# A four-layer graph network on one Trainium2 core: edge starts looked up in rows of 200 instead of 800, and a 6 MB store in seven pieces

## The chip, the core and the metric

The kernel runs on one core of one Trainium2 chip. That core has five engines that each work through their own instruction stream in order: TensorE (PE, matrix products), VectorE (DVE), ScalarE (ACT), GpSimd (POOL) and SyncE (SP, which here only issues transfers). Sixteen DMA engines move data between the chip's memory (HBM) and the core's on-chip memory. SP and ACT issue ordinary transfers; POOL issues the indirect ones, the gathers.

The metric is the time on the device in microseconds, from the start to the end of one execution. Before the change it was 6752.54 us, the median of three runs (6749.43 to 6761.02).

## The reference

There are 6250 nodes with 128 features and 100,000 edges (`src`, `dst`). The edges arrive **sorted by `dst`**. Four layers follow one another, each with a residual and a layer norm:

```python
edge_index = jnp.stack([src, dst])
x = _layernorm(x + _L0_gnn_ref(x, edge_index, ...))               # mean over incoming edges, two products, unit norm
x = _layernorm(x + _L1_gnn_ref(x, edge_weight1, ..., edge_type_8)) # one product per relation, weighted sum
x = _layernorm(x + _L2_gnn_ref(x, edge_index, ...))               # five gated steps (GRU), then an MLP
x = _layernorm(x + _L3_gnn_ref(x, edge_index, edge_attr_16, ...)) # edge MLP, sum by src, node MLP
```

The change touches the first layer only, and the preparation ahead of it:

```python
msg = x[src]
summed = jax.ops.segment_sum(msg, dst, num_segments=n)
cnt = jax.ops.segment_sum(jnp.ones((msg.shape[0],), x.dtype), dst, num_segments=n)
mean = summed / jnp.maximum(cnt, 1.0)[:, None]
out = mean @ W_l + b_l + x @ W_r
return out / jnp.maximum(norm, EPS)                               # norm: the length of each row of out
```

Because `dst` is sorted, the edges of a node are one stretch of the list. If the first edge of node n is first(n), its count is first(n+1) - first(n). So counts need no pass over the edges, only the first edge of each node: the number of `dst` entries below n.

## The kernel before

**Preparation** (`gnn_kernel`, lines 2089 to 2273). `dst` lies in on-chip memory as 125 rows of 800. The last entry of each row (`ends`) tells how many rows end below a given node; a product with a column of ones counts them (line 2133), and that is the row in which the node's first edge lies. Six gathers (line 2141) fetch that row for 6 x 128 nodes, an accumulating compare (`less`, line 2144) counts the entries below the node, and row x 800 + count is the first edge. These starts go to memory (`start_d`) and serve as addresses later. Beside it, x is cut into three bf16 parts in thirteen tiles (`xin`, lines 2254 to 2270), loaded through the SP queue.

**Layer 0** (`even`, lines 777 to 1156). Nodes are cut into steps of four and two tiles of 128. The eight steps of four tiles are *dense*: for each, a 6272 x 512 adjacency matrix of edge counts is built on chip (`stage`, two buffers), written to HBM for the five steps of layer 2 (`adj_d`), and multiplied with x. I call the work on one of them a *chunk*. The rest is *sparse*: its messages are gathered edge by edge (`m<-x_in`, 306 gathers).

The work of the four engines PE, DVE, ACT and POOL is in an order written out by hand: each piece is an event with a due time in units of one chunk, and `play` (line 720) emits the events sorted by it. SP is not among the four; its transfers are placed by the scheduler. A wait in one event holds up everything behind it on its engine. The events are:

- `subtile` (line 940): chunk d spends times d to d+1 on 43 subtiles of twelve nodes. `hot_keys` on DVE makes one-hot matrices `ohk` for one subtile ahead, PE multiplies them with `ohs` (`adj_p`, line 951), ACT copies the sums to `stage` (line 953).
- `block_load` and `block_keys` (lines 906 and 918): every eleven subtiles form a block. SP loads its edge records (`recs`, eleven small transfers), DVE makes `ohs` from them in one long instruction (line 928). The first two blocks are both loaded and keyed ahead of everything else.
- `stored` (line 957), at d+1: SP writes the whole `stage` to HBM in one transfer of 6272 KB.
- `dense0` (line 967), spread over d+1 to d+2: PE multiplies `stage` with x, whose parts `xs` come in groups of seven tiles through SP (`parts_load`, line 960, three buffers; the load of group g+3 is called when group g is used up). `post` then finishes the nodes of the chunk.
- `sparse0` (line 996): one product per gather; the gather is called eight products ahead (`fetch0`), with ten buffers.
- `counts` (line 840): for seven groups of 7 x 128 nodes, 0.37 apart and so within the first 2.7 chunks. `row` finds the row as above; `look` gathers it on POOL (128 rows of 3200 bytes, two buffers `grow`); `less` on DVE compares it, 0.095 of a chunk after its `look`; `first`, `following` and `inverse` make 1/count (`rc`), which `post` needs.

Of the kernel before, what the change touches and what calls it, by code (L numbers as in the profile page):

```python
# [8 lines left out]
F32 = mybir.dt.float32  # L9
BF16 = mybir.dt.bfloat16  # L10
# [5 lines left out]
P = 128  # L16
# [22 lines left out]
SLOTS = 18  # L39
NU = (N + U - 1) // U  # L40
QR = P - 1
NQ = 5 * QR
# [618 lines left out]
def even(ctx: ExitStack, tc: tile.TileContext, a, out, rec_d, start_d, list_d, x_in, ends):  # L661
# [115 lines left out]
    with tc.tile_pool(name="f0", bufs=1) as l0, \  # L777
# [39 lines left out]
        def list_locs(i):  # L817
# [10 lines left out]
        nc.gpsimd.iota(node7, pattern=[[1, CN * P]], base=0, channel_multiplier=0, allow_small_or_imprecise_dtypes=True)  # L828
        ends7 = l0.tile([EP, NT // CN], F32, name="ends7")
        nc.gpsimd.iota(ends7, pattern=[[-CN * P, NT // CN]], base=0, channel_multiplier=0,  # L830
                       allow_small_or_imprecise_dtypes=True)
        nc.vector.tensor_scalar(ends7, ends7, ends, None, op0=ALU.add)
        ones_c = l0.tile([P, 1], BF16, name="ones_c")
# [3 lines left out]
        nc.sync.dma_start(node_d[NPAD:].rearrange("(o p) -> o p", o=1), tail)  # L837
        dst_v = a["dst"].rearrange("(p c) -> p c", p=EP)

        def counts(b, at, to):  # L840
# [3 lines left out]
            def row():  # L844
                ended = l0.tile([EP, CN * P], BF16, tag="ended", name=f"ended{b}")
                nc.vector.tensor_scalar(ended, node7, ends7[:, b:b + 1], None, op0=ALU.is_gt)
                p = ps(f"row_p{b}")
                for j in range(CN):
                    nc.tensor.matmul(p[:, j:j + 1], ended[:, j * P:(j + 1) * P], ones_c[:EP, :], start=True, stop=True)
                v["row"] = row_f = l0.tile([P, CN], F32, tag="row_f", bufs=2, name=f"row_f{b}")  # L850
                nc.vector.tensor_scalar(row_f, p[:, :CN], float(EP - 1), None, op0=ALU.min)
                v["row_i"] = row_i = l0.tile([P, CN], I32, tag="row_i", bufs=2, name=f"row_i{b}")
                nc.vector.tensor_copy(row_i, row_f)
                v["in"] = l0.tile([P, CN], F32, tag="inrow", bufs=2, name=f"inrow{b}")

            def look(j):
                v[j] = g = l0.tile([P, EC], I32, tag="grow", bufs=2, name=f"grow{b}_{j}")
                gather(g, dst_v, v["row_i"][:, j:j + 1])
# [7 lines left out]
            def first():  # L866
                f = l0.tile([P, CN], F32, tag="first", name=f"first{b}")
                nc.vector.scalar_tensor_tensor(f, v["row"], float(EC), v["in"], op0=ALU.mult, op1=ALU.add)
                p = ps(f"first_p{b}")
                nc.tensor.transpose(p[:CN, :P], f, ident)  # L870
                v["T"] = fT = l0.tile([CN, P], F32, tag="firstT", bufs=3, name=f"firstT{b}")
                nc.vector.tensor_copy(fT, p[:CN, :P])
                nc.sync.dma_start(node_d[CN * P * b:CN * P * (b + 1)].rearrange("(t p) -> t p", p=P), fT)
# [16 lines left out]
            for j in range(CN):  # L890
                ev += [(at + 0.06 + 0.05 * j, lambda j=j: look(j)), (at + 0.155 + 0.05 * j, lambda j=j: less(j))]
            return ev + [(at + 0.50, first), (to + 0.12, following), (to + 0.24, inverse)]

# [62 lines left out]

        def stored(d):
            nc.sync.dma_start(adj_d[d].rearrange("p (t n) -> p t n", n=DW), stages[d][:, :NT, :])

# [141 lines left out]
        with tc.manual_schedule(engines=FOUR):  # L1101
            list_load(0)
            for i in range(2):
                block_load(i)
            list_load(1)
            load_weights()
            for i in range(2):
                block_keys(i)
            list_locs(0)
            for k in range(8):  # L1110
                fetch0(k)
# [7 lines left out]
            for d in range(len(dense)):  # L1119
                mine = [o for o in order if o[0] == d]  # L1120
                for k, (_, b, u) in enumerate(mine):
                    t = d + (k + 0.5) / len(mine)
                    g = order.index((d, b, u))
                    nxt = order[g + 1][1:] if g + 1 < len(order) else None
                    i = [x[1] for x in blocks].index(b)
                    if u == 0 and i:
                        events.append((t - 1e-6, lambda i=i: block_load(i + 1)))
                    if u == 7 and i:
                        events.append((t - 2e-6, lambda i=i: block_keys(i + 1)))
                    events.append((t, lambda d=d, b=b, u=u, nxt=nxt: subtile(d, b, u, nxt)))  # L1130
                events.append((d + 1, lambda d=d: stored(d)))
                for s in range(NT):
                    events.append((d + 1 + (s + 0.5) / NT, lambda d=d, s=s: dense0(d, s)))
                events += post(dense[d], d + 2.02, d + 2.95 if d < 7 else d + 2.5)
            for b in range(NT // CN):
                events += counts(b, 0.01 + 0.37 * b, 0.01 + 0.37 * min(b + 1, NT // CN - 1) + 0.50)
            for i in range(1, len(sparse)):
# [937 lines left out]
def gnn_kernel(ctx: ExitStack, tc: tile.TileContext, a, out):  # L2075
# [7 lines left out]
    x_in = dram.tile([NPAD, 3 * D], BF16, name="x_in")  # L2083
    ends = keep.tile([EP, 1], F32, name="ends")
    bad_i = keep.tile([1, 1], I32, name="bad_i")
# [3 lines left out]
    with tc.tile_pool(name="prep", bufs=1) as prep, \  # L2089
# [37 lines left out]
        nc.vector.tensor_copy(d_f, d_i)  # L2127
        nc.vector.tensor_copy(ends, d_f[:, EC - 1:EC])
        ended = prep.tile([EP, NR * P], BF16, name="ended")
        nc.vector.tensor_scalar(ended, node[:EP, :], ends, None, op0=ALU.is_gt)  # L2130
        p_r = psum.tile([P, 512], F32, name="p_r")
        for r in range(NR):
            nc.tensor.matmul(p_r[:, r:r + 1], ended[:, r * P:(r + 1) * P], ones_b[:EP, :], start=True, stop=True)
        row_f = prep.tile([P, NR], F32, name="row_f")
        nc.vector.tensor_scalar(row_f, p_r[:, :NR], float(EP - 1), None, op0=ALU.min)
        row_i = prep.tile([P, NR], I32, name="row_i")
        nc.vector.tensor_copy(row_i, row_f)
        inrow = prep.tile([P, NR], F32, name="inrow")
        for r in range(NR):
            g = prep.tile([P, EC], I32, tag="grow", bufs=NR, name=f"grow{r}")  # L2140
            nc.gpsimd.indirect_dma_start(out=g, out_offset=None, in_=dst_v,
                                         in_offset=bass.IndirectOffsetOnAxis(ap=row_i[:, r:r + 1], axis=0))
            less = prep.tile([P, EC], BF16, tag="less", bufs=2, name=f"less{r}")
            nc.vector.tensor_scalar(less, g, own[:, r:r + 1], 0.0, op0=ALU.is_lt, op1=ALU.add,
                                    accum_out=inrow[:, r:r + 1])
        first = prep.tile([P, NR], F32, name="first")
        nc.vector.scalar_tensor_tensor(first, row_f, float(EC), inrow, op0=ALU.mult, op1=ALU.add)
        p_t = psum.tile([P, 512], F32, name="p_t")
# [169 lines left out]
```

## Time and profile before

| what | value |
|---|---|
| median of three runs | 6752.54 us |
| the profiled execution: its time, and its span from first to last instruction | 6750.44 us, 6748.6 us |
| preparation, until the last write of `x_in` is issued | 0 to 72.6 us |
| first product of a subtile | 102.96 us |
| the eight stores of the adjacency are issued at | 174.1, 283.9, 391.8, 477.9, 559.9, 639.2, 722.2, 804.7 us |
| end of layer 0 (last product of `fhw_p`) | about 895 us |
| gathers `grow` in layer 0: count, first and last issue | 49, 103.8 and 352.9 us |

How to read it: the page names an instruction by line, engine, operation and the tiles it writes and reads ("out<-in"). Busy time is the time of the instructions themselves; idle time ahead of an instruction is put down to what released it ("<-"). The granted clock is the share of full speed that TensorE was allowed. Between two stores lies one chunk, so the table of stores is also a table of chunk lengths: 109.8 and 107.9 us for the second and third, 79.3 to 86.1 us for the later ones.

### The profile page before, as it was taken

Reading aid. Unit: us, or ns where it says so; the run is one execution under the profiler, and the core shown is the slowest. Engines: PE = TensorE matmul, PEld = TensorE weight load, DVE = VectorE, ACT = ScalarE, POOL = GpSimd, SP = SyncE. Lnnn points to the kernel's source line nnn. Section 1 sums busy time; section 2 is a strip of 40 time slices with the busy share of each in tenths; the row PEclk is TensorE's granted clock in tenths of the full one; section 3 lists DMA queues with packets and bytes.
Section 4 is the critical chain, followed back from the end, with each engine's and each line's share of the span. In section 5 each row is a group of like instructions: output and inputs, shape, how many; then the busy total and the mean of one; then the engine's idle time right before and its main releaser. Section 6 shows DMA issues by size and latency. Waiting matters only on the chain.

```text
span 6748.6 us, 83991 instructions
## 1 busy us (share of the span) xinstructions
PE 5859.5 (87%) x25874; PEld 4036.2 (60%) x25874; DVE 2935.8 (44%) x8837; ACT 2404.4 (36%) x3623; POOL 4285.6 (64%) x4463
## 2 busy tenths in 40 slices
PE   4689877789859889999999989999999987888888
PEld 2345445556546657666676667666676665566665
DVE  6676534466624422222222222222222235677776
ACT  2244411111126643333333333333333323444444
POOL 5555447777756656656666666666666622777775
PEclk7899976677769989999999999999999999999999
DMA  5788744444468888768777787778776743444443
GB/s 156 235 246 241 224 135 141 137 135 133 128 179 269 272 284 264 250 221 287 257 255 233 243 301 254 245 227 305 229 239 218 232 155 103 105 107 108 111 107 81
DMA packets 804341, 1358.23 MB, mean 201 GB/s; under 512 B 165559, under 2 KB 428845, under 8 KB 802860
## 3 DMA queue, kind: packets, MB, share of 16 engines
q1 hardware_dynamic: 548348, 693.60, 32.3%
q0 software_dynamic: 207952, 570.83, 28.5%
q10 hardware_dynamic: 47584, 88.33, 3.5%
q8 instruction: 212, 3.47, 0.2%
q14 instruction: 245, 2.01, 0.1%
HBM read 1048.97 MB, written 303.32 MB: 200 GB/s over the span
## 4 chain that ended last, share of the span: by engine, by line
PE 57%; DMA 22%; DVE 8%; issue 5%; POOL 4%; ACT 1%; SPq 1%; DVEq 0%; ACTq 0%; POOLq 0%; another core or an unknown queue 0%
PE ag_p L1445 17%; DMA m<-tab,src_l 7%; PE r L1529 5%; PE z L1529 5%; DMA f_m<-by_dst,f_ix 5%; PE sp_p L1477 4%; DMA fm<-f_hw,turned_hw 4%; PE sum L1366 4%; PE h L1529 3%; PE i L1529 3%; PE ag_p L972 3%; POOL f_m L752 2%; PE adj_p L951 2%; PE g_rank L2037 2%; DMA ab<-adj_d 1%
## 5 line engine op out<-in xcount | busy, mean ns | idle before, releaser
L1445 PE MATMUL ag_p<-af,hs 128*128 128x512 f32 x7056 | 2097.0, 421 | 85.5 <-DMA ab<-adj_d 36.1
L752 POOL DMA_INDIRECT m<-tab,src_l x1530 | 1476.6, 965 | 1055.4 <-PE ag_p L1445 507.5
L1445 PEld LDWEIGHTS ag_p<-af,hs 128*128 128x128 f32 x7056 | 1325.6, 193 | 493.5 <-issue 134.7
L1416 ACT CAST af<-ab 128x1024 fp32r<-128x1024 bf16 (+1 forms) x1000 | 1022.6, 1028 | 984.1 <-PE ag_p L1445 628.5
L752 POOL DMA_INDIRECT f_m<-by_dst,f_ix x819 | 792.2, 967 | 301.8 <-issue 168.2
L752 POOL DMA_INDIRECT fm<-f_hw,turned_hw x782 | 779.6, 997 | 249.1 <-issue 95.5
L1614 POOL DMA_INDIRECT rec_d<-f_rec,row x782 | 778.2, 995 | 237.9 <-issue 207.5
L1477 PE MATMUL sp_p<-m,s 128*128 128x512 f32 (+1 forms) x1530 | 682.3, 446 | 165.8 <-DMA m<-tab,src_l 160.0
L1467 DVE TENSOR_SCALAR s<-iota_h,loc_l 128x128 fp32r<-128x128 f16 x1530 | 421.7, 302 | 769.9 <-PE sp_p L1477 766.1
L1366 PE MATMUL sum<-fs,fm 128*128 128x128 f32 (+13 forms) x1924 | 461.4, 380 | 185.7 <-DMA fm<-f_hw,turned_hw 109.3
L1366 PEld LDWEIGHTS sum<-fs,fm 128*128 128x128 f32 x1924 | 377.1, 272 | 305.9 <-DVE fs L1357 128.1
L752 POOL DMA_INDIRECT m<-x_in,src_l x306 | 349.2, 1141 | 254.7 <-PE sp_p L1003 149.5
L1477 PEld LDWEIGHTS sp_p<-m,s 128*128 128x128 f32 x1530 | 294.5, 192 | 339.6 <-issue 192.7
L953 ACT CAST stage<-adj_p 128x600 bf16<-128x600 f32 (+1 forms) x344 | 224.5, 654 | 347.3 <-PE adj_p L951 313.7
L972 PE MATMUL ag_p<-stage,xs 128*128 128x512 bf16 x1176 | 330.2, 394 | 16.8 <-DMA xs<-x_in 13.4
L951 PE MATMUL adj_p<-ohk,ohs 128*128 128x300 bf16 x1376 | 251.5, 308 | 89.1 <-DVE ohk L936 88.1
L1543 DVE SCALAR_TENSOR_TENSOR r<-h,fc_b_hh,r 128x256 f32<-128x256 f32 (+2 forms) x170 | 101.7, 600 | 521.2 <-PE h L1529 456.4
L1860 ACT ACTIVATE f_hs<-dT,fc_eb 128x512 f32<-128x512 f32 (+1 forms) x208 | 148.8, 715 | 497.3 <-DVE dT L1858 497.3
L1551 ACT ACTIVATE z<-z,f_brz 128x256 f32<-128x256 f32 (+2 forms) x170 | 96.6, 568 | 592.0 <-PE z L1529 531.3
L1336 ACT COPY f_rec<-ap_p 128x512 f32<-128x512 f32 x196 | 105.1, 589 | 561.6 <-issue 335.6
L1357 DVE TENSOR_SCALAR fs<-f_iota_n,loc,turned_wgt 128x128 f32<-128x128 f32 x782 | 245.7, 360 | 92.0 <-PE sum L1366 91.1
L1560 DVE TENSOR_TENSOR r<-hold,ng 128x256 f32<-128x256 f32 (+2 forms) x153 | 84.4, 552 | 459.2 <-ACT ng L1553 459.2
(383 smaller groups left out, 9079.6 us busy)
## 6 DMA issues: line engine op xcount, KB each, us to landing
ab<-adj_d SPq DMA_DIRECT2D x960, 256.0 KB
f_rec<-edge_d SPq DMA_DIRECT2D x391, 130.0 KB
rg<-rec_d SPq DMA_DIRECT2D x195, 260.0 KB
edge_d<-f_rec SPq DMA_DIRECT2D x97, 520.0 KB
adj_d<-stage SPq DMA_DIRECT2D x8, 6272.0 KB
tab<-r ACTq DMA_DIRECT2D x196, 256.0 KB
hs<-tab SPq DMA_DIRECT2D x28, 1792.0 KB
xs<-x_in SPq DMA_DIRECT2D x56, 672.0 KB
```

The source lines that it names most:

```text
L752: nc.gpsimd.indirect_dma_start(out=dst, out_offset=None, in_=table, in_offset=bass.IndirectOffsetOnAxis(ap=idx, axis=0))
L951: nc.tensor.matmul(p[:, q * 512:q * 512 + KH * U], ohss[b][:, 2 * u + j, :], ohk[:, q * KH * U:(q + 1) * KH * U], start=(j == 0), stop=(j ...
L953: nc.scalar.copy(stages[d][:, :, c:c + w].rearrange("p (q b) d -> p q b d", q=2), p.rearrange("p (q n) -> p q n", q=2)[:, :, :KH * U] .rea ...
L972: nc.tensor.matmul(sums["d", d], parts[d, g][:, s % XG, q, :], stages[d][:, s, :], start=(s == 0 and q == 0), stop=(s == NT - 1 and q == 2))
L1357: nc.vector.tensor_scalar(s, iota_n, loc[:, k:k + 1], wgt[:, k:k + 1], op0=ALU.is_equal, op1=ALU.mult)
L1366: nc.tensor.matmul(sums[c][:, x0 - c0:x1 - c0], msg, s[:, x0 - w0:x1 - w0], start=False, stop=(k == last_k[c]))
L1416: nc.scalar.copy(af[:, :m, :], abs_.pop((layer, d, g))[:, :m, :])
L1445: nc.tensor.matmul(sums[layer, d, k], hs[:, s, q, k, :], afs[layer, d, g][:, s % SG, :], start=(s == 0 and q == 0), stop=(s == NT - 1 and ...
L1467: nc.vector.tensor_scalar(s, iota_h, loc_l[:, i, j:j + 1], None, op0=ALU.is_equal)
L1477: nc.tensor.matmul(p[:, :2 * w], hot.pop((layer, k)), msgs.pop((layer, k))[:, :2 * w], start=(j == 0), stop=(j == SLOTS - 1))
L1529: nc.tensor.matmul(p[:, :n], w[:, k, ms], src, start=(start and i == 0), stop=(stop and i == len(ks) - 1))
L1614: st = nc.gpsimd.indirect_dma_start(out=rec3_d, out_offset=bass.IndirectOffsetOnAxis(ap=row3[:, c:c + 1], axis=0), in_=recs[c // CB][:, c ...
```

## The change

Four edits in layer 0, and the first of them also in the preparation:

1. The rows of the look-up hold 200 entries instead of 800. There are now four times as many row ends, so `row` makes four compares instead of one (two buffers) and 28 products instead of seven, which add up in PSUM on top of a product with zeros. A gather brings 800 bytes per row instead of 3200, and `less` runs over 200 entries. In the preparation: four compares, 24 products, six gathers of 200.
2. `grow` has six buffers instead of two, and `less(j)` comes 0.28 of a chunk after `look(j)` instead of 0.095. `first` moves from 0.50 to 0.66, and `following` and `inverse` move with it.
3. `stored` writes seven groups of seven tiles (896 KB each), at d+1, d+1.13, ... d+1.78.
4. At the start only block 0 is keyed, after the first sparse list; the records of block 1 are loaded after the second list, and its keys are made at subtile 7 of block 0.

```diff
+RL = 200
+RQ = EC // RL
...
-        ends7 = l0.tile([EP, NT // CN], F32, name="ends7")
+        ends7 = l0.tile([EP, RQ, NT // CN], F32, name="ends7")
...
+        zero_c = l0.tile([P, CN], F32, name="zero_c")
+        nc.vector.memset(zero_c, 0.0)
...
-        dst_v = a["dst"].rearrange("(p c) -> p c", p=EP)
+        dst_v = a["dst"].rearrange("(r c) -> r c", c=RL)
...
             def row():
-                ended = l0.tile([EP, CN * P], BF16, tag="ended", name=f"ended{b}")
-                nc.vector.tensor_scalar(ended, node7, ends7[:, b:b + 1], None, op0=ALU.is_gt)
                 p = ps(f"row_p{b}")
-                for j in range(CN):
-                    nc.tensor.matmul(p[:, j:j + 1], ended[:, j * P:(j + 1) * P], ones_c[:EP, :], start=True, stop=True)
+                nc.tensor.matmul(p[:, :CN], ident, zero_c, start=True, stop=False)
+                for q in range(RQ):
+                    ended = l0.tile([EP, CN * P], BF16, tag="ended", bufs=2, name=f"ended{b}_{q}")
+                    nc.vector.tensor_scalar(ended, node7, ends7[:, q, b:b + 1], None, op0=ALU.is_gt)
+                    for j in range(CN):
+                        nc.tensor.matmul(p[:, j:j + 1], ended[:, j * P:(j + 1) * P], ones_c[:EP, :],
+                                         start=False, stop=(q == RQ - 1 and j == CN - 1))
...
             def look(j):
-                v[j] = g = l0.tile([P, EC], I32, tag="grow", bufs=2, name=f"grow{b}_{j}")
+                v[j] = g = l0.tile([P, RL], I32, tag="grow", bufs=6, name=f"grow{b}_{j}")
                 gather(g, dst_v, v["row_i"][:, j:j + 1])
...
             for j in range(CN):
-                ev += [(at + 0.06 + 0.05 * j, lambda j=j: look(j)), (at + 0.155 + 0.05 * j, lambda j=j: less(j))]
-            return ev + [(at + 0.50, first), (to + 0.12, following), (to + 0.24, inverse)]
+                ev += [(at + 0.06 + 0.05 * j, lambda j=j: look(j)), (at + 0.06 + 0.28 + 0.05 * j, lambda j=j: less(j))]
+            return ev + [(at + 0.66, first), (to + 0.12, following), (to + 0.24, inverse)]
...
-        def stored(d):
-            nc.sync.dma_start(adj_d[d].rearrange("p (t n) -> p t n", n=DW), stages[d][:, :NT, :])
+        def stored(d, g):
+            ts = slice(XG * g, XG * (g + 1))
+            nc.sync.dma_start(adj_d[d].rearrange("p (t n) -> p t n", n=DW)[:, ts, :], stages[d][:, ts, :])
...
             list_load(0)
-            for i in range(2):
-                block_load(i)
+            block_load(0)
             list_load(1)
+            block_load(1)
             load_weights()
-            for i in range(2):
-                block_keys(i)
             list_locs(0)
+            block_keys(0)
...
-                    if u == 7 and i:
+                    if u == 7:
                         events.append((t - 2e-6, lambda i=i: block_keys(i + 1)))
...
-                events.append((d + 1, lambda d=d: stored(d)))
+                for g in range(NT // XG):
+                    events.append((d + 1 + 0.13 * g, lambda d=d, g=g: stored(d, g)))
...
-                events += counts(b, 0.01 + 0.37 * b, 0.01 + 0.37 * min(b + 1, NT // CN - 1) + 0.50)
+                events += counts(b, 0.01 + 0.37 * b, 0.01 + 0.37 * min(b + 1, NT // CN - 1) + 0.66)
...
-        nc.vector.tensor_scalar(ended, node[:EP, :], ends, None, op0=ALU.is_gt)
+        for q in range(RQ):
+            ended = prep.tile([EP, NR * P], BF16, name=f"ended{q}")
+            nc.vector.tensor_scalar(ended, node[:EP, :], ends[:, q:q + 1], None, op0=ALU.is_gt)
+            eds.append(ended)
...
         for r in range(NR):
-            g = prep.tile([P, EC], I32, tag="grow", bufs=NR, name=f"grow{r}")
+            g = prep.tile([P, RL], I32, tag="grow", bufs=NR, name=f"grow{r}")
```

## The prediction

> **What bounds the kernel now.** The change ends with layer 0, so I read the first 900 us, and first by chunk: busy time of each engine from the first subtile to the first store, and between stores. Columns: length; busy us (instructions) of PE, weight loads, DVE, ACT, POOL; granted clock; DMA share; GB/s.
>
> ```profile
> 102.70:174.10 71.40, 43.07 (x223) 21.84 (x224) 59.28 (x164) 28.09 (x44) 47.49 (x42) 0.76 0.65 174
> 174.10:283.90 109.80, 77.55 (x405) 40.89 (x405) 76.77 (x219) 32.18 (x53) 62.89 (x59) 0.85 0.73 225
> 283.90:391.80 107.90, 82.32 (x430) 45.31 (x428) 77.03 (x229) 39.44 (x68) 58.65 (x53) 0.91 0.77 233
> 391.80:477.90 86.10, 79.78 (x433) 45.04 (x432) 57.81 (x180) 40.20 (x70) 45.17 (x39) 0.98 0.78 232
> 477.90:559.90 82.00, 75.85 (x414) 43.02 (x412) 55.92 (x175) 38.23 (x67) 44.58 (x37) 0.98 0.83 244
> ```
>
> From the fourth chunk on PE is busy 93% of the time and sets the pace. The first three hold the same kind of work, and in the second and third PE is idle for 26 to 32 us. They are the ones with the look-ups. The list of waits from 100 to 400 us (total, times, longest) says on what:
>
> ```profile
> PE adj_p L951 <- DVE ohk L936: 66.3, 28, 14.4
> DVE grow L863 <- DMA grow<-in_dst,row_i: 47.8, 11, 15.0
> POOL grow L752 <- DVE grow L863: 33.2, 10, 13.8
> ```
>
> PE waits for DVE's one-hots; DVE stands in `less` for a gather 47.8 us; POOL, with two buffers, stands for `less`, and its message gathers behind it. The two long waits follow a store directly. In the timeline (start, duration, idle before), with the store on SP's queue:
>
> ```profile
> 174.12 0.32 SPq L958 DMA_DIRECT2D adj_d<-stage  x1
> ...
> 175.01 0.94 POOL L752 DMA_INDIRECT grow<-in_dst,row_i  x1 [0.31 <-issue]
> ...
> 194.64 1.05 DVE L863 TENSOR_SCALAR_CACHE_REDUCE grow<-grow,own_n 128x800 int32<-128x800 int32 x1 [14.74 <-DMA grow<-in_dst,row_i]
> ...
> 196.04 1.18 PE L951 MATMUL adj_p<-ohk,ohs 128*128 128x300 bf16 x4 [14.36 <-DVE ohk L936]
> ```
>
> So a gather behind a store takes 19.6 us to land, and its wait reaches PE. The same happens to an `xs` load at the last store:
>
> ```profile
> 804.71 0.33 SPq L958 DMA_DIRECT2D adj_d<-stage  x1
> 805.13 7.73 SPq L964 DMA_DIRECT2D xs<-x_in  x2
> ...
> 832.44 1.46 PE L972 MATMUL ag_p<-stage,xs 128*128 128x512 bf16 x3 [12.68 <-DMA xs<-x_in]
> ```
>
> **The change, part by part.**
>
> *Later compare, six buffers, chunks one to three.* By form, DVE's waits for `grow` were 8.6, 22.5 and 16.6 us in the three chunks. A lag of 0.28 chunk is 17 us in a chunk of 62 and 24 us in one of 85; the worst landing seen is 19.6 us with four times the bytes. I take all three waits as gone. Buffer j-6 is compared 0.02 before `look(j)`, so POOL waits little.
>
> *Shorter compare.* 49 `less` at 1.037 us over 800 entries. The row for 128 elements (`fo`, L1049) has 0.345 us; the line through both gives 0.42 for 200, so 0.62 less each: 9.9, 12.4 and 8.7 us of DVE for 16, 20 and 14.
>
> *Four compares and 28 products per `row`.* Three more compares at 0.458 us. With two buffers the third waits for PE's products of the first, so PE and DVE go hand in hand: two compares of 0.46, a handover of 0.3 (102.46 to 102.77 us), products at about 0.05 each and the zero product near `inv_p`'s 0.23: some 1.5 us more per row, between 0 (hidden by the subtile that DVE is ahead) and 2.5 (every handover exposed). I take 1.5: 3, 4.5 and 1.5 us for the rows after the first.
>
> *Keys of block 1* move into chunk one: 3.3 us of DVE there (L924 and L928).
>
> Sums: 71.4-8.6-9.9+3+3.3 = 59.2; 109.8-22.5-12.4+4.5 = 79.4; 107.9-16.6-8.7+1.5 = 84.1 us. Other engines set floors. POOL keeps its number of gathers, each with 0.30 us between them: 47.5+42x0.3 = 60.1, 62.9+59x0.3 = 80.6 and 74.6 us. On top comes a hand-over of a port:
>
> ```profile
> 125.39 3.08 DVE L928 TENSOR_TENSOR ohs<-iota_h,recs 128x2816 bf16<-128x2816 f16 x1
> 125.92 3.37 POOL L752 DMA_INDIRECT m<-x_in,src_l  x1 [0.30 <-issue]
> ```
>
> A gather whose issue takes 0.95 us took 3.37 while DVE made `ohs`. The Trainium skill ("SBUF — State Buffer", "Who interferes with whom") says that DVE in a two-port mode locks GpSimd out of the port pair used for writing gather descriptors, `tensor_scalar` among its cases. That speaks against the change: `ended` may be such an instruction, and there are 21 more. By the rule they cost POOL up to 21x0.46 = 9.7 us; by the rows (`ended` at 121.71 beside a 1.04 us gather) almost nothing. I take 4 us of it in chunk two, and 2.3 for the additional `ohs` in chunk one: 62 and 85. Chunk three is PE's: 82.3 at the fourth chunk's 92.7% gives 88. Together 235 against 289.1: **-54.1 us**. Below all this, DVE would need some 195.
>
> *Start.* Before, DVE was through the second block's keys at 100.3 and the first subtile ran at 102.96. The first block's records were there at 89.45 and its `ohs` done at 92.6; the same 2.3 us of one-hots and `row`, plus 1.5 for the longer row, give 96.6: **-6.4 us**. The second block's records are needed at subtile 7, about 106; SP needs 6.75 us per block (22 in 13.50) and 2.6 for the list, so they are issued by 99.
>
> *Preparation.* DVE stood 5.9 us for the first row of 800, which landed 9.43 us after issue; six compares of 0.62 go; 3 x 0.53 for `ended` and about 1 for 18 products come, ahead of the gathers. The starts and the records, behind which SP issues the last `xin` loads, come some 5 us earlier. The order here is not fixed by hand: between -6 and +3, I take **-4 us**.
>
> *Store in seven.* The fills (L1154) show how SP is placed: due at 1.5, 3.5 and 4.5 chunks, they were issued at 171.46, 378.52 and 462.60 us, which is 0.96, 2.88 and 3.82. What waits for nothing goes out about 0.55 early. So pieces 0 to 4 go together when the stage is full, and only two of seven move: 1.83 MB at the 280 GB/s of this stretch is **-6.6 us** of the 12.68. It is 0 if all seven go together, and -12.7 if they spread. Here a rule opposes: "DMA: Bandwidth & Descriptors" ("Anatomy of one DMA") fits a transfer (there one that GpSimd issues) at 2.0 us plus bytes by 436 GB/s, so seven pieces in series would cost 28.7 instead of 16.7 us, 96 us over eight stores. The rows speak for overlap: SP issues a store in 0.32 us and the next load 0.4 us later. Only the buffer's next use two chunks on waits for a piece; I take nothing.
>
> Sum: 4+6.4+54.1+6.6 = 71.1 us off the profiled execution's 6750.4 (span 6748.6 and 1.8 around it), which is 2.1 below the median: 6752.5-71.1 = **6681 us**.
>
> **Rivals.**
>
> *Gathers still late.* In the shorter first chunk the lag is 17 us, and landing behind five pieces at once may take as long. For it: landing follows the queue, not the gather's size. Against: five sevenths of the store, a quarter of the bytes. If half of the 54 stays, 6708.
>
> *POOL sets the pace.* Its floors of 60 and 81 lie close to my chunks. With the full lock and no benefit from fetching eight ahead, the chunks are 66, 92 and 90: a gain of 41 in place of 54.1, and 6694; with -4 and -6.6 failing too, 6705.
>
> *More.* Rows hidden, PE at 93% of its busy time, the whole `xs` wait gone: 55, 78 and 86 us, and 6650.
>
> *Given back.* If PE was going to wait for messages or records anyway, only start and end remain, about 10 us, and that is within 0.2%: 6743.
>
> *Slower: the stage buffer.* The last piece is due at d+1.78; ACT's first copy into that buffer at d+2.01, 19 us later. A piece takes 3.3 us at 280 GB/s. SP goes in order and has stood up to 15.1 us at one pair of `f_hw` writes (561.46). From 15.6 us behind, ACT, then PE, wait at six chunk borders. It decides from 14 us each ((71+13.5)/6); at 18 us, 6x18-71 = +37: 6790. Against it: loads and fills go early, not late.
>
> **How the numbers follow.** No change can be told from one within 0.2%, 13.5 us. My forecast has 0.60, own range 6655 to 6705; late gathers 0.10; POOL 0.10; more 0.08; given back 0.05; slower 0.07. The faster cases sum to 0.88. The range leaves out the last two cases, part of "more" and the end of the late gathers: 6645 to 6730.
>
> **What would show it.** Right: no wait of `less` for `grow` over 3 us, POOL hardly waiting for `less`, stores beginning near 158, 243 and 331 us, later chunks at 79 to 86 us as before, first subtile near 92 (96.6 less the preparation's 4). Wrong: PE idle for DVE at the four-compare rows by over 3 us, POOL without a gap in chunk two, ACT waiting for a piece of the store.

## The result

The changed kernel takes 6679.5 us (median of four runs, 6674.4 to 6684.0). The kernel before took 6751.0 us in the same comparison. The ratio is 0.9893, with a 95% interval of 0.9876 to 0.9910: about 71.5 us less. The profiled execution took 6684.0 us, with a span of 6682.2, so its span is 66.4 us shorter than that of before.

| us | before | after | difference |
|---|---|---|---|
| last write of `x_in` issued | 72.62 | 73.75 | +1.1 |
| first product of a subtile | 102.96 | 97.16 | -5.8 |
| to the first store (chunk one) | 71.2 | 55.6 | -15.6 |
| chunk two | 109.8 | 87.6 | -22.2 |
| chunk three | 107.9 | 92.4 | -15.5 |
| chunk four | 86.0 | 92.4 | +6.4 |
| chunks five to eight | 326.9 | 323.9 | -3.0 |
| last store to the end of layer 0 | 90.4 | 76.2 | -14.2 |
| end of layer 0 | 895.1 | 825.2 | -69.9 |
| the rest of the kernel | 5853.5 | 5857.0 | +3.5 |

The whole gain lies inside layer 0. The 3.5 us in the rest, which runs the same instructions in both kernels, is what two profiled executions differ by without a cause in the change.

The busy time by chunk of the changed kernel has the columns of the first table in the prediction: the stretch and its length; PE, weight loads, DVE, ACT and POOL; granted clock, DMA share, GB/s.

```profile
97.00:152.70 55.70, 41.23 (x268) 24.12 (x269) 53.27 (x166) 28.16 (x44) 43.31 (x36) 0.84 0.54 125
152.70:240.30 87.60, 72.63 (x455) 41.44 (x463) 66.18 (x221) 31.03 (x51) 69.62 (x60) 0.93 0.73 206
240.30:332.70 92.40, 81.80 (x450) 46.03 (x458) 70.42 (x238) 39.62 (x69) 65.98 (x57) 0.96 0.84 239
332.70:425.10 92.40, 81.33 (x427) 45.62 (x434) 60.76 (x188) 40.45 (x71) 44.81 (x40) 0.96 0.78 219
425.10:507.60 82.50, 75.87 (x414) 43.39 (x422) 56.95 (x179) 39.75 (x70) 44.97 (x39) 1.00 0.84 244
```

In chunk one DVE is busy for 53.3 of 55.7 us and waits for no other engine or transfer over 0.5 us: DVE sets the pace there, with POOL close behind (43.3 us for 36 gathers and 36 gaps of 0.30 are 54.1). In chunk two PE is idle for 15 us (32 before), but look at POOL: 60 gathers busy for 69.62 us, and 60 gaps of 0.30 between them are 18 more, together 87.6 us, the whole length of the chunk. In chunk three PE is busy 89% of the time.

The granted clock rose too, from 0.76, 0.85 and 0.91 in the first three chunks to 0.84, 0.93 and 0.96. PE is busy 72.6 us in chunk two, with 50 more (short) products than in the 77.6 us before. What part of the gain comes with the clock is not shown.

The list of waits of the changed kernel from 97 to 330 us, for all engines (total, times, longest):

```profile
PE adj_p L958 <- DVE ohk L943: 22.7, 12, 3.0
...
PE sp_p L1011 <- DMA m<-x_in,src_l: 5.9, 7, 1.4
...
DVE ended L853 <- PE row_p L855: 5.6, 2, 4.0
...
POOL grow L754 <- DVE grow L870: 2.1, 6, 0.6
```

There is no line of DVE waiting for `grow` any more (47.8 us before). POOL's wait for `less` fell from 33.2 to 2.1 us, and PE's wait for one-hots from 66.3 to 22.7. (Both lists take in the first three chunks and no wait of these kinds outside them.) New are a short wait of PE for gathered messages and one of DVE for the products of `row`.

SP's issues at the last store of the changed kernel (start, duration, how many in a row):

```profile
749.01 0.33 SPq L966 DMA_DIRECT2D adj_d<-stage  x1
749.44 0.39 SPq L972 DMA_DIRECT2D xs<-x_in  x1
749.87 2.13 SPq L966 DMA_DIRECT2D adj_d<-stage  x2
756.81 0.37 SPq L972 DMA_DIRECT2D xs<-x_in  x1
757.22 2.71 SPq L966 DMA_DIRECT2D adj_d<-stage  x2
...
767.18 0.78 SPq L966 DMA_DIRECT2D adj_d<-stage  x1
...
776.89 0.37 SPq L966 DMA_DIRECT2D adj_d<-stage  x1
```

The pieces go out over 28 us, with the `xs` loads between them. The first load stands behind one piece instead of the whole matrix, and PE's wait for `xs`, 12.68 us before, is gone.

### The profile page after: what moved, and what is told of

It reads as the page before. It is cut to its first block, busy times and chain, and to the rows that moved or that the text cites. A ratio compares the mean times of both kernels' runs of the same rounds, so it can differ in the third digit from the quotient of the medians.

```text
span 6682.2 us, 84263 instructions
## 1 busy us (share of the span) xinstructions
PE 5830.8 (87%) x25895; PEld 4035.8 (60%) x26053; DVE 2913.0 (44%) x8862; ACT 2404.6 (36%) x3623; POOL 4290.3 (64%) x4463
## 4 chain that ended last, share of the span: by engine, by line
PE 59%; DMA 21%; DVE 8%; issue 5%; POOL 4%; ACT 2%; SPq 1%; DVEq 0%; ACTq 0%; POOLq 0%
PE ag_p L1453 17%; DMA m<-tab,src_l 7%; PE r L1537 5%; PE z L1537 5%; DMA fm<-f_hw,turned_hw 4%; DMA f_m<-by_dst,f_ix 4%; PE sp_p L1485 4%; PE sum L1374 4%; PE h L1537 3%; PE i L1537 3%; PE ag_p L980 3%; PE adj_p L958 2%; POOL f_m L754 2%; PE g_rank L2045 1%; DMA ab<-adj_d 1%
## 5 line engine op out<-in xcount | busy, mean ns | idle before, releaser
L1453 PEld LDWEIGHTS ag_p<-af,hs 128*128 128x128 f32 x7056 | 1326.3, 193 | 492.8 <-issue 133.4
L980 PE MATMUL ag_p<-stage,xs 128*128 128x512 bf16 x1114 | 310.2, 386 | 7.1 <-ACT aT L987 3.2
L1874 PE MATMUL m_p<-f_hs,fw_L_gnn_eW 128*128 128x512 f32 (+1 forms) x416 | 227.2, 629 | 66.4 <-ACT mT L1876 64.1
```

The costliest lines, as they stand in the source:

```text
L980: nc.tensor.matmul(sums["d", d], parts[d, g][:, s % XG, q, :], stages[d][:, s, :], start=(s == 0 and q == 0), stop=(s == NT - 1 and q == 2))
L1453: nc.tensor.matmul(sums[layer, d, k], hs[:, s, q, k, :], afs[layer, d, g][:, s % SG, :], start=(s == 0 and q == 0), stop=(s == NT - 1 and ...
L1874: nc.tensor.matmul(p_m[:, :e], e2[:, 0, :], held[i].pop("hs")[:, :e], start=True, stop=True)
```

## The experiments

The kernels ran in three groups, each on one chip, and each is compared with the kernel before on its own chip. On the chips of the second and third groups the kernels take 14 to 15% longer than on the first (the last section has more of this), so only ratios, or profiles within a group, are compared. The profiles of the first group are set beside those of the result above; whether that is the same chip is not on record, but the kernel before takes as long on both (6747.9 and 6751.0 us). "From the first subtile" means from the first product of a subtile to the end of layer 0: 792.2 us before and 728.0 after, 64.1 less. The only profile of the kernel before is that of the result.

| kernel | group | ratio to the kernel before | from the first subtile, us |
|---|---|---|---|
| changed, store in one | 1 | 0.9937 (0.9918 to 0.9955) | 746.1 |
| changed, `less` early | 1 | 0.9929 (0.9910 to 0.9947) | 743.3 |
| before, rows of 200 alone | 1 | 0.9979 (0.9972 to 0.9986) | 771.8 |
| changed, counts 0.50 apart | 1 | 0.9890 (0.9871 to 0.9909) | 723.8 |
| before, store in seven alone | 2 | 0.9936 (0.9913 to 0.9960) | 771.1 |
| before, start alone | 2 | 0.9977 (0.9960 to 0.9994) | 801.6 |
| changed, preparation of before | 2 | 0.9941 (0.9919 to 0.9963) | 767.2 |
| changed, seven pieces at d+1 | 2 | 0.9931 (0.9909 to 0.9953) | 774.0 |
| the same again | 3 | 0.9948 (0.9927 to 0.9969) | 772.9 |
| changed kernel itself | 3 | 0.9943 (0.9924 to 0.9962) | 770.8 |
| changed, `ohs` in four | 3 | 0.9951 (0.9934 to 0.9968) | 760.8 |
| three edits together | 3 | 0.9930 (0.9911 to 0.9950) | 774.7 |

### The store in one transfer again

The changed kernel with edit 3 undone.

```diff
-        def stored(d, g):
-            ts = slice(XG * g, XG * (g + 1))
-            nc.sync.dma_start(adj_d[d].rearrange("p (t n) -> p t n", n=DW)[:, ts, :], stages[d][:, ts, :])
+        def stored(d):
+            nc.sync.dma_start(adj_d[d].rearrange("p (t n) -> p t n", n=DW), stages[d][:, :NT, :])
...
-                for g in range(NT // XG):
-                    events.append((d + 1 + 0.13 * g, lambda d=d, g=g: stored(d, g)))
+                events.append((d + 1, lambda d=d: stored(d)))
```

> The changed kernel, with the store of a chunk in one piece again. Theory (the split store saves the wait for xs at the last store and little else): PE waits for xs some 13 us at the last store again, layer 0 ends 7 to 14 us later, chunks one to eight stay within 3 us each, total +7 to +14 us over the changed kernel. Rival (the look-ups were late because they stood behind the single store, and the split is what cured them): DVE waits for grow of 10 us or more come back after the stores of the first three chunks, total +25 us or more.

Measured: 6700.4 us, and the end of layer 0 comes 17.4 us later than in the changed kernel. That is more than the 7 to 14 us of the theory. The part after the last store takes 12.4 us more, and the `xs` wait of 12.5 us is back. `less` waits for no `grow`: the lag alone covers the landing, even behind a whole store. But chunk two takes 95.0 us instead of 87.6, for which the theory had no term. The timeline of this kernel behind its first store:

```profile
154.12 0.33 SPq L965 DMA_DIRECT2D adj_d<-stage  x1
...
172.74 0.48 PE L1010 MATMUL sp_p<-m,s 128*128 128x384 bf16 x1 [13.36 <-DMA m<-x_in,src_l]
...
177.54 0.82 DVE L853 TENSOR_SCALAR ended<-node,ends 125x896 bf16<-125x896 f16 x2 [17.06 <-PE row_p L855]
```

With the look-ups out of the way, a message gather stands behind the store: PE waits 13.36 us for it (1.4 us at most in the changed kernel), and `row` waits behind PE. So the store in pieces gains at two places, at the last store and at the message gathers, and neither theory had named the second.

### `less` early again

The changed kernel with the lag of edit 2 undone; six buffers and short rows stay.

```diff
-                ev += [(at + 0.06 + 0.05 * j, lambda j=j: look(j)), (at + 0.06 + 0.28 + 0.05 * j, lambda j=j: less(j))]
-            return ev + [(at + 0.66, first), (to + 0.12, following), (to + 0.24, inverse)]
+                ev += [(at + 0.06 + 0.05 * j, lambda j=j: look(j)), (at + 0.155 + 0.05 * j, lambda j=j: less(j))]
+            return ev + [(at + 0.50, first), (to + 0.12, following), (to + 0.24, inverse)]
...
-                events += counts(b, 0.01 + 0.37 * b, 0.01 + 0.37 * min(b + 1, NT // CN - 1) + 0.66)
+                events += counts(b, 0.01 + 0.37 * b, 0.01 + 0.37 * min(b + 1, NT // CN - 1) + 0.50)
```

> The changed kernel, but less comes 0.095 of a chunk after look again, and first at 0.50; rows of 200, six buffers and the split store stay. Theory (the lag removes the waits): DVE waits for grow several us in total in the first three chunks, total +10 to +30 us. Rival (rows of a quarter of the bytes, six buffers and the split store land in time anyway, the lag is not needed): no wait over 1 us, total within 4 us.

Measured: 6695.1 us; layer 0 ends 15.9 us later. The waits of this kernel in its first three chunks:

```profile
PE adj_p L958 <- DVE ohk L943: 35.3, 19, 8.6
...
DVE grow L870 <- DMA grow<-in_dst,row_i: 20.1, 5, 6.8
```

DVE stands 20.1 us for `grow`, and PE's wait for one-hots is 12.6 us longer (22.7 in the changed kernel, each over its own first three chunks). Chunks one and two take 63.8 and 97.6 us instead of 55.6 and 87.6; chunk four takes 86.2 instead of 92.4. This is the theory's mechanism, and the last number shows its price: the later due times push work into chunk four.

### Rows of 200 alone

The kernel before with edit 1 and nothing else (`row` in four compares, two buffers of 200, the compare early).

```diff
...
-                v[j] = g = l0.tile([P, EC], I32, tag="grow", bufs=2, name=f"grow{b}_{j}")
+                v[j] = g = l0.tile([P, RL], I32, tag="grow", bufs=2, name=f"grow{b}_{j}")
...
```

> The kernel before with rows of 200 alone: two buffers, the short lag, one store, both blocks keyed at the start. Theory (size is a smaller part than lag and buffers): the waits of DVE for grow stay at half or more of 47.8 us, those behind the stores above all; total -15 to -35 us. Rival (bytes decide): waits of DVE for grow under 10 us, total -45 us or more.

Measured: a ratio of 0.9979, about 14 us, and 20.3 us from the first subtile. The waits of this kernel:

```profile
DVE grow L870 <- DMA grow<-in_dst,row_i: 40.0, 8, 10.5
POOL grow L754 <- DVE grow L870: 19.4, 10, 6.1
```

A quarter of the bytes takes only 7.8 us off the 47.8 us that DVE waits, as the theory had it: the gather's own size is the smaller part. What takes the rest off is the lag or the cut store, as the other runs show.

### Counts 0.50 apart

The changed kernel with the seven groups of look-ups further apart, so that fewer of POOL's gathers fall into chunk two.

```diff
-                events += counts(b, 0.01 + 0.37 * b, 0.01 + 0.37 * min(b + 1, NT // CN - 1) + 0.66)
+                events += counts(b, 0.01 + 0.50 * b, 0.01 + 0.50 * min(b + 1, NT // CN - 1) + 0.66)
```

> The changed kernel, with the seven groups of counts 0.50 chunk apart instead of 0.37, so that the same 49 gathers are spread over 3.5 chunks. Theory (POOL sets the pace of chunk two, with no free time there): chunk two falls from 87.6 by 4 to 8 us, chunk three by 0 to 4, the fourth grows by 0 to 3, total -4 to -10 us. Rival (DVE and PE set it): the same work only moves between chunks, the sum of the first five stays within 2 us.

Measured: chunk two takes 79.2 us instead of 87.6, chunk three 89.9 instead of 92.4, chunk four 96.0 instead of 92.4. The stretch of chunk two in this kernel:

```profile
152.00:231.20 79.20, 68.78 (x439) 39.84 (x444) 65.29 (x205) 32.15 (x53) 62.64 (x55) 0.96 0.78 221
```

POOL has 55 gathers: 62.64 and 55 x 0.30 are 79.1 us, again the length of the chunk. Neither here nor in the changed kernel does POOL stand for longer than 0.35 us in this chunk. So POOL sets the pace of chunk two in the changed kernel: with five gathers fewer the chunk is shorter, and again as long as POOL's work. Layer 0 ends 3.5 us earlier; the whole time, 0.9890 against 0.9893, doesn't tell the two kernels apart.

### Store in seven alone, and start alone

Two kernels, each the one before with one edit: the store as in edit 3, and the start as in edit 4.

```diff
             list_load(0)
-            for i in range(2):
-                block_load(i)
+            block_load(0)
             list_load(1)
+            block_load(1)
             load_weights()
-            for i in range(2):
-                block_keys(i)
             list_locs(0)
+            block_keys(0)
...
-                    if u == 7 and i:
+                    if u == 7:
```

> The kernel before with the store in seven pieces alone. Theory: the 12.7 us wait for xs at the last store goes, the two DVE waits of 14 to 15 us for grow behind the stores shrink to 3 to 8, total -15 to -30 us. Rival (a transfer cut in seven pays seven fixed costs, and the queue is busier): the waits stay, total within 5 us or slower.

> The kernel before with the new start alone: one block keyed ahead. Theory: first subtile 6 to 8 us earlier, 3 us given back in chunk one, total -3 to -8 us. Rival (chunk one stands in waits for gathers, which come at their own time): the first store is issued no earlier than before, total within 2 us.

Measured: the store alone has a ratio of 0.9936, which is 49 us of 7726 (31 to 67) and more than the 15 to 30 that were expected. The start alone has 0.9977. With the new start the first subtile comes at 96.44 us instead of the 102.67 of the store's kernel, 6.2 us earlier; the gain of 0.23% (0.06 to 0.40) is 18 us, with an interval that holds 6. Whether the first store came earlier for it, as its rival denies, can't be read without a profile of before on that chip. With the store in seven, chunks one to three take 282.4 us against 303.3 with the new start alone, and the `xs` wait is gone. DVE's waits for `grow` in the kernel with the store in seven:

```profile
DVE grow L863 <- DMA grow<-in_dst,row_i: 20.2, 7, 6.4
```

In the kernel with the start alone they are 35.6 us. So cutting the store also takes much of the look-ups' wait: two edits act on the same wait, and their gains don't add up.

### Preparation of before

The changed kernel with rows of 800 in the preparation only.

```diff
-            g = prep.tile([P, RL], I32, tag="grow", bufs=NR, name=f"grow{r}")
+            g = prep.tile([P, EC], I32, tag="grow", bufs=NR, name=f"grow{r}")
...
         first = prep.tile([P, NR], F32, name="first")
-        nc.vector.scalar_tensor_tensor(first, row_f, float(RL), inrow, op0=ALU.mult, op1=ALU.add)
+        nc.vector.scalar_tensor_tensor(first, row_f, float(EC), inrow, op0=ALU.mult, op1=ALU.add)
```

> The changed kernel with the preparation of before (rows of 800, one compare), the rest as changed. Forecast of record (short rows save 4 us of preparation): the last write of x_in is issued 3 to 6 us later than in the changed kernel, total +4 us. Rival (seen in the trace: the starts are written earlier, but the last xin loads follow the records, which come no earlier): the preparation ends within 2 us of the changed kernel's or up to 2 us earlier, total within 3 us.

Measured: the last write of `x_in` is issued at 71.84 us, against 73.60 in the changed kernel with its pieces at d+1 on the same chip. The whole time doesn't tell them apart. Over all profiles, the nine with short rows in the preparation have 73.3 to 74.5 us there, the five with rows of 800 have 71.5 to 72.9: the short rows make the preparation about 1.8 us longer. The changed kernel's own timeline says where it goes:

```profile
34.72 0.28 SPq L2168 DMA_DIRECT2D start_d<-at_i  x1
...
58.80 0.30 SPq L2258 DMA_DIRECT2D rec_d<-rec  x1
59.20 0.37 SPq L2271 DMA_DIRECT2D xin<-in_x  x1
```

and that of the kernel before:

```profile
38.51 0.28 SPq L2155 DMA_DIRECT2D start_d<-at_i  x1
...
54.92 0.30 SPq L2245 DMA_DIRECT2D rec_d<-rec  x1
55.31 1.12 SPq L2258 DMA_DIRECT2D xin<-in_x  x2
```

The starts are written 3.8 us earlier, as forecast. The records are written 3.9 us later, and an `xin` load waits behind them on SP.

### All seven pieces due at d+1

Does the cut do it, or that the pieces are spread?

```diff
-                    events.append((d + 1 + 0.13 * g, lambda d=d, g=g: stored(d, g)))
+                    events.append((d + 1 + 1e-7 * g, lambda d=d, g=g: stored(d, g)))
```

> The changed kernel with the seven pieces of a store all due at once, at d+1. Theory (what counts is that other transfers get between the pieces): like one store again, PE waits for xs 5 to 13 us at the last store, total +4 to +12 us. Rival (the cut itself, into transfers of 896 KB, is what helps): within 3 us of the changed kernel.

Measured: 0.9931, and an `xs` wait of 3.0 us. The changed kernel did not run on this chip, so the pair was measured on a third one.

> The changed kernel with the seven pieces of a store all due at d+1, now beside the changed kernel. Theory (other transfers must get between the pieces): PE waits 3 to 13 us for xs at the last store, total +4 to +12 us over the changed kernel. Rival (the cut itself is enough): within 3 us.

> The changed kernel itself, beside the three others of this call. All expect 0.988 to 0.991 of the kernel before, no wait for grow, and seven pieces spread over a chunk.

Measured: 0.9948 against 0.9943 for the changed kernel, which are not told apart. From the last store to the end of layer 0 it is 81.3 us against 76.5. SP at the last store with all pieces due at once:

```profile
789.22 0.33 SPq L966 DMA_DIRECT2D adj_d<-stage  x1
789.65 0.39 SPq L972 DMA_DIRECT2D xs<-x_in  x1
790.08 5.86 SPq L966 DMA_DIRECT2D adj_d<-stage  x6
797.02 0.37 SPq L972 DMA_DIRECT2D xs<-x_in  x1
```

The load that PE needs first goes out behind one piece even here; the second one goes out behind all seven, and PE waits 2.9 us. The cut alone brings most of it; the spreading brings 4.8 us at the end of layer 0, of which 2.1 are left from the first subtile (772.9 against 770.8). The changed kernel's own 0.9943 lies outside the 0.988 to 0.991 that were expected.

### `ohs` in four, and three edits together

Is it `ohs` that holds up the gathers' issue? The changed kernel with the one-hots of a block made in four parts, at the last four subtiles of the block before; and the same with the counts 0.50 apart and the preparation of before.

```diff
-            nc.vector.tensor_tensor(ohs[:, :2 * n, :], iota_h.unsqueeze(1).to_broadcast([P, 2 * n, P]),
+            nc.vector.tensor_tensor(ohs[:, js, :], iota_h.unsqueeze(1).to_broadcast([P, w, P]),
...
+                    if u >= n_of[b] - 4:
+                        events.append((t - 1.5e-6, lambda i=i, s=u - n_of[b] + 4: block_part(i + 1, s)))
```

> The changed kernel, with the long instruction that makes ohs (L928 before, 3.1 us, four in a chunk) cut into four pieces, at the last four subtiles of a block. Theory (POOL, held up in a gather for the length of ohs, sets the pace of chunk two, and in the later chunks PE waits about 3 us for ohk behind ohs once or twice): no gather takes over 2 us, chunk two falls by 3 to 8 us, the later chunks by 1 to 3 each, total -8 to -25 us. Rival (both waits are covered elsewhere): within 4 us.

> The changed kernel with ohs in four pieces, the counts 0.50 chunk apart, and the preparation of before (rows of 800). Theory: the three gains add up, preparation -1.5 to -2 us, counts apart -2 to -6, ohs as in its own run; total -12 to -30 us against the changed kernel. Rival (with ohs cut POOL has room, and the spreading gives nothing more): equal to the kernel with ohs cut alone, within 4 us.

Measured: 0.9951 and 0.9930, against 0.9943 of the changed kernel on the same chip; neither is told apart from it. The groups of the kernel in four, over layer 0 (count, busy us, mean ns of one):

```profile
L754 POOL DMA_INDIRECT m<-x_in,src_l x298 | 310.6, 1042 | 295.4 <-PE sp_p L1024 178.2 <-PE adj_p L971 73.0 <-issue 28.3
...
L946 DVE TENSOR_TENSOR ohs<-iota_h,recs 128x768 bf16<-128x768 f16 x93 | 88.4, 951 | 0.0
```

and those of the changed kernel on that chip:

```profile
L754 POOL DMA_INDIRECT m<-x_in,src_l x298 | 341.9, 1147 | 261.6 <-PE sp_p L1011 153.7 <-PE adj_p L958 63.0 <-issue 32.4
...
L935 DVE TENSOR_TENSOR ohs<-iota_h,recs 128x2816 bf16<-128x2816 f16 x23 | 70.9, 3082 | 0.0
```

The same 298 gathers take 31.3 us less of POOL, for 14.1 us more of DVE (107.5 us in all its `ohs` against 93.4). So it is `ohs` that stretches them. From the first subtile layer 0 is 10.0 us shorter in the profile, but twelve runs don't show it in the whole time: as a gain it stays unproved. Chunks one and two are 6 us shorter each; the later ones together are not, which the theory had expected, and three gathers of the first three chunks still take over 2 us. In the kernel with all three edits the gains don't add up: its median lies 6.7 us below the changed kernel's instead of 12 to 30, and from the first subtile it takes 774.7 us.

## Why the prediction was right

The forecast was 6681 us with a range of 6645 to 6730; 6679.5 was measured. The sum is right because its main term, the chunks with the look-ups, came out as forecast; some terms around it are wrong and cancel, and the main term's own parts are in part luck.

- **Waits of `less` gone in chunks one to three: right.** The three chunks take 55.6 + 87.6 + 92.4 = 235.6 us, where the forecast had 235. The waits for `grow` went to nothing, and undoing the lag brings 20.1 us of them back. The forecast split of the sum was wrong, though (62, 85, 88): errors of -6.4, +2.6 and +4.4 us cancel. And the prediction gave the store no part in these waits. The kernels with the store in seven alone (20.2 us of them) and with the start alone (35.6) show that it has one, and behind a whole store a message gather held up PE by 13.36 us.
- **POOL as a floor of chunk one: wrong.** That floor counted 42 gathers and 62 us; only 36 fell into the 55.7 us. Most of the rest came in chunk three (57 gathers, 53 before). That PE went on from the messages fetched ahead is likely, but not shown. Chunk two is POOL's to the last microsecond, not by more gathers (60, 59 before) but by longer ones (69.6 us of issues, 62.9 before). Over both chunks POOL fills 43.3 + 69.6 + 96 x 0.30 = 141.7 of 143.3 us. This was the rival "POOL sets the pace", and it happened in chunk two, at a smaller price than the rival's 92.
- **The shorter compare: right.** 0.42 us was forecast, and 49 took 410 ns each.
- **Four compares per `row`: right for the first, mis-sized behind it.** From PE's first product of the first `row` to the first subtile it is 1.48 us (95.68 to 97.16), 0.19 before (102.77 to 102.96): 1.3 us more, where 1.5 were forecast. In chunk two, DVE stood 3.95 us before the third compare. The timeline of the changed kernel there:

```profile
160.11 0.32 PE L1011 MATMUL sp_p<-m,s 128*128 128x384 bf16 x1 [1.34 <-DMA m<-x_in,src_l]
...
163.82 0.82 DVE L853 TENSOR_SCALAR ended<-node,ends 125x896 bf16<-125x896 f16 x2 [3.95 <-PE row_p L855]
164.90 1.16 PE L958 MATMUL adj_p<-ohk,ohs 128*128 128x300 bf16 x4
```

  The upper bound of 2.5 us assumed that PE comes to the row's products at once; PE had been held up by message gathers (1.34 and 0.92 us) and had other products ahead of them. Over the three chunks DVE's wait is 5.6 us in two places.
- **The port: a hold-up there is, but the allowance was for the wrong instruction.** 4 us were set aside for `ended` in chunk two, of at most 9.7. Gathers whose issue took over 1.5 us are 10 before and 16 after in the first three chunks; 12 of these 16 lie beside the 12 `ohs` of that stretch, 3 beside `ohk`, and one, of 1.66 us, beside `ended`. A count from 1.5 us up would miss a hold-up by one `ended` of 0.46, so the shorter ones count too: the twelve gathers beside an `ended` and no `ohs` take 1.11 us in the mean, against 0.95 for one that nothing holds up, some 2 us in all. The rule that the prediction cites names `tensor_scalar`, which `ended` is; the long hold-ups are by `ohs`, a `tensor_tensor`, and the measurement decides. What POOL paid is in `grow`, before and after:

```profile
L752 POOL DMA_INDIRECT grow<-in_dst,row_i x49 | 52.7, 1076 | 86.1 <-DVE grow L863 33.2 <-DVE s L994 14.7 <-DVE row_i L853 14.1
L754 POOL DMA_INDIRECT grow<-in_dst,row_i x49 | 64.2, 1310 | 23.5 <-DVE ohk L943 10.4 <-issue 4.3 <-DVE grow L870 2.1
```

  That is 11.5 us more, because more of them now meet `ohs`. The 2.3 us for the additional `ohs` in chunk one were charged to the right instruction.
- **Chunk four "as before": wrong by 6.4 us.** The later due times move two of the seven `inverse` out of chunk three. Of the waits of the changed kernel between 332.7 and 425.1 us:

```profile
PE inv_p L893 <- DVE invT L891: 4.4, 2, 2.8
```

  With `less` early this wait is gone, and chunk four takes 86.2 us. With the store in one the wait is there (4.5 us), though the stores lie 87.2 us apart: fewer products fall between those two stores. So the lag costs the 4.4 us; the other 2 are PE's busy time. The forecast moved the waits away and didn't ask what the moved events meet.
- **Start: right.** 6.4 us were forecast; the first subtile is 5.8 us earlier, 6.9 without the preparation's 1.1, and 6.2 with the start alone.
- **Preparation: wrong sign.** -4 us were forecast, inside bounds of -6 to +3; it is +1.1 here and about +1.8 over all profiles. The failed step is that the starts and the records "come some 5 us earlier": the starts did (3.8 us), the records came 3.9 us later. The records are not computed from the starts; their place is the scheduler's, and why it is later is not shown.
- **Store: mis-sized, 14.2 instead of 6.6 us.** The step read from the fills that five pieces would go out together. They went out as 1, 2, 2, 1 and 1, with a load behind the first; the forecast's end "if they spread", 12.7, is what happened. With all due at once, 2.9 of the 12.5 us of waiting are left: the load's place behind the first piece counts most. The estimate that opposed it, 96 us more for pieces in series, did not come: with the store in one again layer 0 takes 18.1 us more.

The errors: preparation 5.1 worse, chunk four 6.4, chunks one to three 0.8 and the rest of the kernel 3.5 worse; store 7.6, chunks five to eight 3.0 and the start 0.5 better. Together they are 4.7 us: 66.4 less in the profile, where 71.1 were forecast. That the median comes within 2 us all the same is luck, since the profiled execution lies 4.5 us above its median.

Three sums of the prediction are slightly off and decide nothing: 82.3 at 92.7% is 88.8 and not 88, its compares per chunk add up to 50 for 49, and its case "More" comes to 6659 by its own terms, not 6650.

Of the signs named for a right forecast, two failed: the first subtile came at 97.2 us and not near 92, and chunk four took 92.4 us and not 79 to 86. Of those for a wrong one, "POOL without a gap in chunk two" appeared. So a total near the forecast did not mean that every step was as forecast.

Three rivals did not happen. "Gathers still late": no wait of `less` is left. "Given back": chunks one to three kept 53.3 us. "The stage buffer": in all of layer 0 no wait of ACT for a piece of the store is seen.

What stays open is how the gain splits between lag and store. Undone singly from the whole, the store costs 18.1 us from the first subtile and the lag 15.3; the rows alone bring 20.3. On the second chip the store in seven alone takes 771.1 us from the first subtile, no more than the kernels with nearly all edits (767.2 and 774.0), and its ratio is like theirs (0.9936; 0.9941 and 0.9931): there the other edits added nothing that is seen. The store alone was not run on the first chip.

## What to carry to other kernels

A large store issued in one piece can delay what is issued behind it, on other queues too (here a look-up, a load and a message gather, by 12 to 15 us each). Where small transfers that an engine waits for follow it, cutting it is worth a try. Here a wait on an in-order engine was removed by distance between issue and use more than by a smaller transfer, but the events that were moved back cost something where they arrived. When several edits serve the same wait, their single gains don't add up, and the next engine (here POOL, by busy time plus its gap times the number of gathers) shows how far the sum can go.

## What the runs showed of the hardware

**A gather issued while `ohs` runs is held until `ohs` ends.** A gather's issue takes 0.95 us by itself. In the layer 0 of before, 26 gathers took over 1.2 us beside an `ohs` (3.08 us long), and each of them ended 0.81 to 0.83 us after it, whenever it had begun; gathers begun over 0.2 us before `ohs` took 0.94 to 1.03 us. In the changed kernel one took 3.23 us, and others up to 4.2. Cut into four, `ohs` left the 298 message gathers at a mean of 1042 ns instead of 1147. The changed kernel's timeline in chunk two:

```profile
167.28 3.08 DVE L935 TENSOR_TENSOR ohs<-iota_h,recs 128x2816 bf16<-128x2816 f16 x1
167.94 3.23 POOL L754 DMA_INDIRECT m<-x_in,src_l  x1 [0.30 <-PE sp_p L1011]
```

**The same program takes 14 to 15% longer on two other chips.** The kernel before has 6747.9, 7725.7 and 7718.2 us on the three. The changed kernel has 6684.0 us in the profile of the result and 7699.2 in the third group; 972.5 of the 1015 us lie after layer 0. The pages' rows of the loop behind layer 0 in the result,

```profile
L1453 PE MATMUL ag_p<-af,hs 128*128 128x512 f32 x7056 | 2100.8, 422 | 86.5 <-DMA ab<-adj_d 35.7
...
L1453 PEld LDWEIGHTS ag_p<-af,hs 128*128 128x128 f32 x7056 | 1326.3, 193 | 492.8 <-issue 133.4
```

and on the third group's chip:

```profile
L1453 PE MATMUL ag_p<-af,hs 128*128 128x512 f32 x7056 | 2185.6, 434 | 380.4 <-issue 209.4
...
L1453 PEld LDWEIGHTS ag_p<-af,hs 128*128 128x128 f32 x7056 | 1363.2, 199 | 842.9 <-issue 395.7
```

One of these matmuls is 3% longer (434 against 422 ns; granted clock 0.864 against 0.921 over the span). The idle time of weight loads that wait for nothing that the profile shows is three times as long (395.7 against 133.4 us). The cause is open. It matters for the reading of gains: on that chip the change is worth 0.57%, not 1.07%, and chunk one takes 77.1 us instead of 55.6.
